# Start of an adapter kernel: block 0's tokens in four loads, its B rows in two gathered halves, row numbers on Pool

## The chip, the core and the metric

The kernel runs on one core of one Trainium2 chip. A core has five engines that run their own instruction streams and meet at semaphores: TensorE (PE, with its weight loads listed apart as PEld), VectorE (DVE), ScalarE (ACT), GpSimd (POOL) and SyncE (SP). Loads and stores are issued by SP or, for gathers through a table of row numbers, by POOL. All of them are carried out by the same 16 DMA engines. The metric is the time of one execution on the device in microseconds (us).

## What is computed

4096 tokens (64 sequences of 64), each of 1024 features, pass two residual layers in float32. The first adds a rank-16 adapter chosen for each sequence. The second adds a dense product with W and a mixture of eight rank-16 adapters with the two best gates.

```python
def reference(x, itok_B_4_50, itok_B_0_7, L0_cond_A, L0_cond_B,
              L1_cond_W, L1_cond_Wr, L1_cond_A, L1_cond_B):
    # layer 0: per sequence, its own adapter
    Bx  = einsum('bni,bri->bnr', x, B0[ids0])
    x   = x + einsum('bnr,bor->bno', Bx, A0[ids0])          # SCALING 1
    # layer 1
    base   = einsum('btd,od->bto', x, W)
    logits = einsum('btd,ed->bte', x, Wr) + 5.0 * one_hot(ids1)
    gates  = softmax over the 2 largest logits, 0 elsewhere
    h      = einsum('btd,erd->bter', x, A1)
    lora   = einsum('bter,bte,eor->bto', h, gates, B1)
    return x + base + 2.0 * lora
```

## The kernel before

Tokens lie along the free axis (`xT` is features by tokens), in 8 blocks of 512 tokens. A block `k` has two tiles of 1 MB, `("x", k, 0)` and `("x", k, 1)`, each with four chunks of 128 features (`HC` = 4). Blocks are taken in pairs. For a pair, the product with W plus the identity is a fast matrix multiplication of seven products at two levels (`products`, lines 817 to 1043), which fills nearly all of TensorE's time.

Before that, each block goes through a preparation, written as small functions:

- `load` (line 366): SP loads the block's two token tiles. `gather` (line 400): POOL gathers 128 rows (eight sequences of rank 16) of B (`gb`) and of A (`ga`) by an indirect DMA, 512 KB each, with row numbers `idx` (line 294).
- `turn` (line 415): TensorE transposes the gathered B in two groups of four 128x128 pieces (`pt`), and ScalarE copies each group to `bt`.
- `project` (line 436): TensorE multiplies `bt` with the tokens (`pb`), in two steps, one for each token tile. VectorE masks the sum into `bx`.
- `adapt` (line 468): TensorE makes the adapter's output (`px`) from `bx` and `ga`, and VectorE adds it to the tokens in place, eight operations a block.
- `rows` (line 506): TensorE makes hidden rows and logits (`ph`) from the tokens and `a1_sb`; then `gates` on VectorE and `weigh` (`pg`) follow.

The first three words of a block's preparation, `turn`, `project` and `adapt`, are called `early`; `rows`, `gates` and `weigh` are `late`.

Nothing of this is issued in the order in which it is written. Each function hands steps to a `Plan` (line 34) with the engine, an estimated duration, what is read and written, a due number `at`, and for DMAs a size. `Plan.order` (line 65) runs a small model of the engines and fixes one order for every engine; `Pinned` (line 19) keeps it. Two kinds of edges exist there: `reads`/`writes` are real dependences, and `behind` only asks that another step has begun. The constants of the model are in lines 44 to 51; `GATHER` is what it adds to a gather's landing. An engine then works in that order and waits in place, so an instruction that waits holds all behind it on its engine.

Two holds are made by hand. A tile's first column is written by a small POOL copy that reads another tile, and the DMA that fills the tile must come after that copy:

```python
pool.tensor_copy(made[t][:, 0, :1], made["x", 0, 0][:, 0, :1])   # line 374: x_0_1's load after x_0_0's first half
pool.tensor_copy(a1_sb[:, 0, :1], made["gb", 0][:, :1])          # line 321: a1's load after the gathered B of block 0
```

SP issues in order, so with `a1`'s load the loads behind it wait as well: the 16 pieces of W (`load_w`, line 637), block 1's tokens and `b1`. Through `behind` block 1's gathers follow too.

In the built program the start stands thus. SP: `ids_sb`, two halves of `x_0_0` (512 KB each), `wr_c`, `ids1_sb`, `x_0_1` (1 MB, waits for POOL's copy), `a1_sb` (waits for POOL's second copy), two pieces of W, `x_1_0`, `x_1_1`, 14 pieces of W, `b1_sb`. POOL: constants, `gb` of block 0, copy for `x_0_1`, `ga` of block 0, copy of `wr_c` into `a1_sb` (line 328), copy for `a1_sb`, `gb` and `ga` of block 1, then sums of weight pieces. TensorE: `pt`, `pb`, `px` of block 0, both groups of `pt` of block 1, `ph` of block 0 (four strips of 128 tokens), `pb` of block 1, then the first product (`pw`) with `px` of block 1 between.

On a second tensor with the same name: the page writes `in_b` for both B tables, `in_a` for both A tables, `ids_sb` for both id tiles, `x` for every token tile and `w` for the pieces of W and for two small gate tiles. All of the kernel's own operations carry line 29, that of the recording helper.

Of the kernel before, what the change touches and what calls it, by code (L numbers as in the profile page):

```python
# [11 lines left out]
ALU = mybir.AluOpType  # L12
AX = mybir.AxisListType

P = 128
# [18 lines left out]
class Plan:  # L34
# [10 lines left out]
    LOOK = 0.2  # L45
    LAND = 1.8
    KB = 350.0
    GATHER = 1.5
    AHEAD = 6.0
    PACE = {"DVE": 0.36, "POOL": 0.73}  # L50
    SET = {"SP": 1.2, "DVE": 3.1, "POOL": 2.9}
# [13 lines left out]
    def order(self):  # L65
# [65 lines left out]
        while ready:  # L131
# [23 lines left out]
            if st["kb"]:  # L155
                moved = max(moved, clock[e]) + st["kb"] / self.KB
                end[n] = (moved if e == "SP" else clock[e] + self.GATHER) + self.LAND
            where[n] = e
# [23 lines left out]
def kernel(  # L182
# [44 lines left out]
    D, NT = xT.shape  # L227
# [7 lines left out]
    TB = 512  # L235
# [3 lines left out]
    RANK = P // BPB  # L239
    NJ = TB // P  # L240
    HC = NC // 2
# [14 lines left out]
    pe, dve = Pinned(tc, nc.tensor), Pinned(tc, nc.vector)  # L256
    act, pool, sp = Pinned(tc, nc.scalar), Pinned(tc, nc.gpsimd), Pinned(tc, nc.sync)
# [6 lines left out]
    plan = Plan(slots, {"l"})  # L264
# [7 lines left out]
    def new(tag, shape, name):  # L272
        return pools[tag].tile(shape, F32, tag=tag, name=name)


    ids_sb = const.tile([P, NBLK], I32, name="ids_sb")
# [5 lines left out]
    rcol = const.tile([P, 1], F32, name="rcol")  # L282
# [8 lines left out]
    dve.tensor_copy(half, half_i)  # L291
    mask = const.tile([P, GT], F32, name="mask")
    idx = const.tile([P, NBLK], I32, name="idx")
    dve.tensor_scalar(idx, ids_sb, float(RANK), rcol, ALU.mult, ALU.add)
    pool.memset(mask[:, :SEQ], 0.0)
    pool.memset(mask[:, SEQ:], float(RANK))

    a1_sb = const.tile([P, NC, P + E], F32, name="a1_sb")
# [10 lines left out]
    dve.tensor_copy(order, order_i)  # L309
    b1_sb = const.tile([P, O], F32, name="b1_sb")  # L310

    def consts():
        plan.add({"SP": 0.4}, lambda e: sp.dma_start(wr_c, wr), [], [("wr_c",)], -53, kb=8)
        plan.add(
            {"SP": 0.4}, lambda e: sp.dma_start(ids1_sb, ids1[0:1, :].to_broadcast([P, NB])),
            [], [("ids1",)], -53, kb=32,
        )

        def hold(e):

            pool.tensor_copy(a1_sb[:, 0, :1], made["gb", 0][:, :1])

        plan.add({"POOL": 0.2}, hold, [(("gb", 0),)], [("a1",)], -56)
        plan.add({"SP": 0.4}, lambda e: sp.dma_start(a1_sb[:, :, :P], a1), [], [("a1",)], -45, kb=512)
        plan.add({"SP": 0.4}, lambda e: sp.dma_start(b1_sb, b1), [], [("b1",)], -29, kb=512, behind=[("a1",)])

        def spread(e):
            pool.tensor_copy(a1_sb[:, :, P:], wr_c)

        plan.add({"POOL": 0.3}, spread, [("wr_c",)], [("wr",)], -45)  # L330
# [24 lines left out]
    made = {}  # L355

    def part(t, cs=range(HC), gs=range(NG)):
        return [(t, c, g) for c in cs for g in gs]
# [7 lines left out]
    def load(k, i, at):  # L366
        t = ("x", k, i)

        held = (k, i) == (0, 1)

        def hold(e):

            made[t] = new("q", [P, HC, TB], f"x_{k}_{i}")
            pool.tensor_copy(made[t][:, 0, :1], made["x", 0, 0][:, 0, :1])


        cuts = ((0, HC // 2), (HC // 2, HC)) if (k, i) == (0, 0) else ((0, HC),)

        def fn(c0, c1):
            if not held and c0 == 0:  # L380
                made[t] = new("q", [P, HC, TB], f"x_{k}_{i}")
            sp.dma_start(
                made[t][:, c0:c1],
                xT[(i * HC + c0) * P : (i * HC + c1) * P, k * TB : (k + 1) * TB].rearrange(
                    "(c p) t -> p c t", p=P
                ),
            )

        if held:
            plan.add(  # L390
                {"POOL": 0.2}, hold, part(("x", 0, 0), [0]), part(t), at, [("q", t)]
            )
        for c0, c1 in cuts:
            plan.add(
                {"SP": 0.5}, lambda e, c0=c0, c1=c1: fn(c0, c1),
                [], part(t, range(c0, c1)), at, [("q", t)] * (not held and c0 == 0),
                kb=256 * (c1 - c0), behind=[("a1",)] * (k == 1) + [(t, 0, 0)] * (c0 > 0),
            )

    def gather(k, tag, table, at):  # L400
        def fn(e):
            made[tag, k] = new(tag, [P, D], f"{tag}_{k}")
            pool.indirect_dma_start(
                out=made[tag, k],
                out_offset=None,
                in_=table,
                in_offset=bass.IndirectOffsetOnAxis(ap=idx[:, k : k + 1], axis=0),
            )

        plan.add(  # L410
            {"POOL": 1.1}, fn, [], [((tag, k),)], at, [(tag, (tag, k))], kb=512,
            behind=[(("x", 0, 1), 0, 0)] * ((tag, k) == ("ga", 0)) + [("a1",)] * (k == 1) + [(("px", 1, 1, 0),)] * (k > 1),
        )

    def turn(k, g, at):

        pt, bt = ("pt", k, g), ("bt", k)

        def fn(e):
            made[pt] = new("l", [P, PER, P], f"pt_{k}_{g}")  # L420
            if g == 0:
                made[bt] = new("bt", [P, NC, P], f"bt_{k}")
            for c in range(PER):
                cc = g * PER + c
                pe.transpose(made[pt][:, c, :], made["gb", k][:, cc * P : (cc + 1) * P], ident)

        def out(e):
            act.copy(made[bt][:, g * PER : (g + 1) * PER, :], made[pt])

        plan.add(  # L430
            {"PE": 0.44}, fn, [(("gb", k),)] + [(bt, 0)] * g, [(pt,)] + [(bt, 0)] * (g == 0), at,
            [("l", pt)] + [("bt", bt)] * (g == 0),
        )
        plan.add({"ACT": 0.6}, out, [(pt,)], [(bt, g + 1)], at)

    def project(k, at):

        pb, bx = ("pb", k), ("bx", k)

        def fn(cs):  # L440
            if cs[0] == 0:
                made[pb] = new("l", [P, GT], f"pb_{k}")
                made[bx] = new("bx", [P, GT], f"bx_{k}")
            for c in cs:
                for gi in range(NG):
                    strip = slice(gi * CG, (gi + 1) * CG)
                    pe.matmul(
                        made[pb][strip, :],
                        made["bt", k][:, c, strip],
                        x_at(k, c)[:, gi * GT : (gi + 1) * GT],  # L450
                        start=(c == 0),
                        stop=(c == NC - 1),
                        tile_position=(0, gi * CG),
                    )

        def out(e):
            dve.tensor_tensor(made[bx], made[pb], mask, ALU.mult)


        for h in range(2):  # L460
            plan.add(
                {"PE": 0.94}, lambda e, h=h: fn(range(h * HC, (h + 1) * HC)),
                [(("bt", k), 1), (("bt", k), 2)] + part(("x", k, h)), [(pb,)] + [(bx,)] * (1 - h),
                at + 0.1 * h, [("l", pb), ("bx", bx)] * (1 - h),
            )
        plan.add({"DVE": 0.3}, out, [(pb,)], [(bx,)], at - 8)

    def adapt(k, h, at):

        px = [("px", k, h, gi) for gi in range(NG)]  # L470

        tags = "aabb" if (k, h) == (0, 1) else "llll"
        x = ("x", k, h)

        def fn(e):
            for gi in range(NG):
                made[px[gi]] = new(tags[gi], [P, HC, GT], f"px_{k}_{h}_{gi}")
            for c in range(HC):
                cc = h * HC + c
                for gi in range(NG):  # L480
                    strip = slice(gi * CG, (gi + 1) * CG)
                    pe.matmul(
                        made[px[gi]][:, c, :],
                        made["ga", k][strip, cc * P : (cc + 1) * P],
                        made["bx", k][strip, :],
                        start=True,
                        stop=True,
                        tile_position=(gi * CG, 0),
                    )

        def out(gi):
            def fn(e):
                xs = made[x][:, :, gi * GT : (gi + 1) * GT]
                dve.tensor_tensor(xs, made[px[gi]], xs, ALU.add)

            return fn

        plan.add(
            {"PE": 1.1}, fn, [(("ga", k),), (("bx", k),)], [(t,) for t in px], at,
            list(zip(tags, px)),  # L500
        )
        for gi in range(NG):
            xs = part(x, gs=[gi])
            plan.add({"DVE": 0.62}, out(gi), [(px[gi],)] + xs, xs, at - 2 + 1.5 * gi * (k == 0))
# [172 lines left out]
    POOL = {"POOL": 1.25}  # L677
# [366 lines left out]

    for k, at in ((0, -60), (1, -42)):
        load(k, 0, at)
        gather(k, "gb", b0, at - 1)
        load(k, 1, at)
        gather(k, "ga", a0, at)
        if k == 0:  # L1050
            consts()
# [81 lines left out]
```

## Time and profile before

| | |
|---|---|
| median of 3 runs | 522.11 us (521.61 to 522.37) |
| the profiled execution | 521.59 us |
| its span, first to last instruction | 519.8 us |
| outside the span in that execution | 1.8 us |
| PE busy | 504.9 us, 97% of the span |
| DVE, POOL, ACT busy | 300.9, 170.0, 41.1 us |
| granted TensorE clock | 1.000 |
| HBM read, written | 69.01 MB, 29.62 MB |

A row of a timeline has the start, the duration (merged where several instructions of one kind follow each other), the engine, the operation and its operands, and in brackets the idle time of the engine before it with what ended it. "SPq" is SP's queue issuing a DMA: the duration there is that of the issue, not of the transfer. A row of the chain of waits has start, duration, engine and tile. A row of the table of windows has the stretch, its length, each engine's busy time with the number of instructions, the granted clock, the share of the 16 DMA engines and the rate in GB/s.

Where this document gives the landing of a DMA, it is the last of the 16 completions that the trace records for it. Where it counts packets, these are the trace's DMA packets by queue (queue 0: POOL's gathers; queue 1: SP's loads and stores), time and size.

### The profile page before, as it was taken

To read this page: it belongs to the slowest core of one execution; us is meant where nothing else is said; L and a number is where in the kernel's file an instruction comes from. 1 tells how busy PE (TensorE), PEld (TensorE's weight loads), DVE (VectorE), ACT (ScalarE), POOL (GpSimd) and SP (SyncE) were. 2 spreads that over 40 slices of the span, in tenths; PEclk is the share of its full clock that TensorE was granted. 3 is DMA by queue.
4 is the path that set the end of the run, shared out by engine and by line. 5 is a ranking of instruction groups with operands and counts; after the bars stand their busy time and mean duration, and the time that the engine had idled before them with its cause. 6 is when DMAs were issued, how large, how long until landed. Compare 5 with 4: busy or idle time off the path is not lost.

```text
span 519.8 us, 8542 instructions
## 1 busy us (share of the span) xinstructions
PE 504.9 (97%) x3432; PEld 439.3 (85%) x3432; DVE 300.9 (58%) x572; ACT 41.1 (8%) x81; POOL 170.0 (33%) x141
## 2 busy tenths in 40 slices
PE   2999999999999999999999999999999999999996
PEld 2857988888888988898888998889888898888885
DVE  0699998986953383526684256435486418433632
ACT  1111100002000100012000100000200010000000
POOL 4072067170332144124233313312423322433300
PEclk9999999999999999999999999999999999999999
DMA  7999276799566269716565537744546633610122
GB/s 263 370 367 381 103 263 221 276 326 342 194 202 203 63 194 317 238 61 204 182 224 186 159 101 212 269 149 124 163 161 202 204 95 107 204 62 0 56 104 83
DMA packets 54247, 99.19 MB, mean 191 GB/s; under 512 B 4928, under 2 KB 11072, under 8 KB 54208
## 3 DMA queue, kind: packets, MB, share of 16 engines
q1 hardware_dynamic: 51904, 90.26, 51.6%
q0 software_dynamic: 2304, 8.39, 4.8%
q8 instruction: 27, 0.44, 0.3%
q14 instruction: 12, 0.10, 0.0%
HBM read 69.01 MB, written 29.62 MB: 190 GB/s over the span
## 4 chain that ended last, share of the span: by engine, by line
PE 96%; DMA 2%; DVE 0%; issue 0%; SPq 0%; POOL 0%
PE pa L29 39%; PE pb L29 38%; PE ph L29 11%; PE px L29 3%; PE pw L29 3%; DMA x<-in_xT 2%; PE pt L29 1%; PE pg L29 1%; DVE o L29 0%; SPq L29 0%; DVE bx L29 0%; POOL x L29 0%
## 5 line engine op out<-in xcount | busy, mean ns | idle before, releaser
L29 PE MATMUL pa<-ti,s 128*128 128x256 f32 x432 | 102.5, 380 | 0.0
L29 PE MATMUL pb<-ti,s 128*128 128x256 f32 x384 | 95.8, 380 | 0.0
L29 PEld LDWEIGHTS pa<-ti,s 128*128 128x128 f32 x432 | 80.8, 190 | 11.2 <-issue 0.2
L29 PEld LDWEIGHTS pb<-ti,s 128*128 128x128 f32 x384 | 72.1, 190 | 10.0
L29 PEld LDWEIGHTS ph<-a_sb,x 128*128 128x128 f32 x512 | 62.6, 190 | 1.5 <-issue 0.4
L29 PE MATMUL ph<-a_sb,x 128*128 128x136 f32 x512 | 63.1, 279 | 0.2 <-issue 0.2
L29 POOL TENSOR_TENSOR ti<-x,ti 128x512 f32<-128x512 f32 x24 | 32.2, 1340 | 78.0 <-PE pb L29 77.1
L29 DVE TENSOR_TENSOR o<-pb,o 128x512 f32<-128x512 f32 x47 | 32.4, 690 | 36.1 <-PE pb L29 21.7
L29 PE MATMUL pa<-x,s 128*128 128x256 f32 x216 | 51.9, 379 | 0.0
L29 POOL TENSOR_TENSOR ti<-t,ti 128x512 f32<-128x512 f32 x18 | 25.7, 1429 | 71.0 <-PE pb L29 61.3
L29 POOL TENSOR_TENSOR ti<-x 128x512 f32<-128x512 f32 x24 | 30.8, 1282 | 55.4 <-PE pb L29 41.8
L29 PEld LDWEIGHTS pa<-x,s 128*128 128x128 f32 x216 | 40.1, 190 | 5.3 <-issue 0.3
L29 DVE TENSOR_TENSOR x<-px,x 128x512 f32<-128x512 f32 x64 | 39.8, 684 | 6.8 <-PE px L29 6.8
L29 PE MATMUL pa<-t,s 128*128 128x256 f32 x168 | 41.0, 380 | 0.0
L29 POOL TENSOR_TENSOR ti<-t 128x512 f32<-128x512 f32 x18 | 24.4, 1358 | 42.9 <-PE pb L29 33.4
L29 PEld LDWEIGHTS pa<-t,s 128*128 128x128 f32 x168 | 31.6, 190 | 4.5 <-issue 0.4
L29 DVE TENSOR_TENSOR o<-pa,u 128x512 f32<-128x512 f32 x32 | 22.0, 688 | 20.8 <-PE pa L29 20.1
L29 DVE TENSOR_TENSOR u<-pb,u 128x512 f32<-128x512 f32 x21 | 14.5, 689 | 25.1 <-ACT u L29 20.7
L29 POOL TENSOR_TENSOR s<-w,w 128x512 f32<-128x512 f32 x12 | 17.0, 1418 | 36.0 <-DVE w L29 36.0
L29 PE MATMUL pb<-hg,b_sb 128*128 128x256 f32 x96 | 28.6, 379 | 0.0
L29 DVE TENSOR_TENSOR o<-pa,v 128x512 f32<-128x512 f32 x15 | 10.3, 690 | 25.9 <-PE pa L29 25.9
L29 DVE TENSOR_TENSOR v<-pa,u 128x512 f32<-128x512 f32 x16 | 11.0, 689 | 22.3 <-PE pa L29 22.1
(113 smaller groups left out, 609.5 us busy)
## 6 DMA issues: line engine op xcount, KB each, us to landing
s<-s_kept SPq DMA_DIRECT2D x147, 256.0 KB
x<-in_xT SPq DMA_DIRECT2D x15, 1024.0 KB
out_T<-o SPq DMA_DIRECT2D x30, 512.0 KB
s_kept<-s SPq DMA_DIRECT2D x28, 256.0 KB
s_kept<-w SPq DMA_DIRECT2D x18, 256.0 KB
w<-in_w SPq DMA_DIRECT2D x16, 256.0 KB
x<-in_xT SPq DMA_DIRECT2D x2, 512.0 KB
out_T<-o SPq DMA_DIRECT2D x4, 256.0 KB
```

What stands on the lines that cost most here:

```text
L29: return self._tc.keep_in_program_order(f(*args, **kwargs))
```

## The change

Block 0's second token tile is no longer held; both tiles come in halves, so that four loads of 512 KB stand behind each other on SP. The hold on `a1_sb` reads the last half of `x_0_1` instead of the gathered B. Block 0's B is gathered by two indirect DMAs, one for each half of the columns (256 KB each), and each group of transposes depends on its own half alone. `idx` is computed by POOL, as its last operation before the gathers. `GATHER` goes from 1.5 to 2.3.

```diff
-    GATHER = 1.5
+    GATHER = 2.3
...
-    dve.tensor_scalar(idx, ids_sb, float(RANK), rcol, ALU.mult, ALU.add)
...
+    pool.tensor_scalar(idx, ids_sb, float(RANK), rcol, ALU.mult, ALU.add)
+
     def consts():
...
-            pool.tensor_copy(a1_sb[:, 0, :1], made["gb", 0][:, :1])
-
-        plan.add({"POOL": 0.2}, hold, [(("gb", 0),)], [("a1",)], -56)
+            pool.tensor_copy(a1_sb[:, 0, :1], made["x", 0, 1][:, HC // 2, :1])
+
+        plan.add({"POOL": 0.2}, hold, part(("x", 0, 1), [HC // 2]), [("a1",)], -56)
...
     def load(k, i, at):
         t = ("x", k, i)
-        held = (k, i) == (0, 1)
-        def hold(e):
-            made[t] = new("q", [P, HC, TB], f"x_{k}_{i}")
-            pool.tensor_copy(made[t][:, 0, :1], made["x", 0, 0][:, 0, :1])
-        cuts = ((0, HC // 2), (HC // 2, HC)) if (k, i) == (0, 0) else ((0, HC),)
+        cuts = ((0, HC // 2), (HC // 2, HC)) if k == 0 else ((0, HC),)
...
     def gather(k, tag, table, at):
-        def fn(e):
-            made[tag, k] = new(tag, [P, D], f"{tag}_{k}")
+        n = 2 if (tag, k) == ("gb", 0) else 1
+        def fn(h):
+            if h == 0:
+                made[tag, k] = new(tag, [P, D], f"{tag}_{k}")
             pool.indirect_dma_start(
-                out=made[tag, k],
+                out=made[tag, k][:, h * D // n : (h + 1) * D // n],
                 out_offset=None,
                 in_=table,
                 in_offset=bass.IndirectOffsetOnAxis(ap=idx[:, k : k + 1], axis=0),
+                element_offset=h * D // n,
             )
+        if n == 2:
+            plan.add(
+                {"POOL": 1.1}, lambda e: fn(0), [], [((tag, k), 0)], at, [(tag, (tag, k))], kb=256
+            )
+            plan.add(
+                {"POOL": 1.1}, lambda e: fn(1), [], [((tag, k), 1)], at, kb=256,
+                behind=[((tag, k), 0)],
+            )
+            return
...
-            {"PE": 0.44}, fn, [(("gb", k),)] + [(bt, 0)] * g, ...
+            {"PE": 0.44}, fn, [(("gb", k), g)] + [(bt, 0)] * g, ...
...
-                [(("bt", k), 1), (("bt", k), 2)] + part(("x", k, h)), ...
+                [(("bt", k), h + 1)] + part(("x", k, h)), ...
...
     for k, at in ((0, -60), (1, -42)):
         load(k, 0, at)
+        load(k, 1, at)
         gather(k, "gb", b0, at - 1)
-        load(k, 1, at)
         gather(k, "ga", a0, at)
```

In the built program this gives, on SP: `ids_sb`, four halves of block 0's tokens, `wr_c`, `ids1_sb`, `a1_sb` (waits for POOL), and from there the same loads as before. On POOL: constants, `idx`, two halves of `gb`, `ga`, the copy for `a1_sb` (waits for the last half of `x_0_1`), `gb` of block 1, the copy of `wr_c`, `ga` of block 1. On TensorE the second group of block 1's transposes stands between the two pairs of `ph` strips instead of before them. One store of a weight piece changes places with its neighbour on SP. From there on the orders are the same.

More of the change, by code (lines that the diff above doesn't have):

```diff
@@ L367, in load @@
         t = ("x", k, i)
-        held = (k, i) == (0, 1)
-        def hold(e):
-            made[t] = new("q", [P, HC, TB], f"x_{k}_{i}")
-            pool.tensor_copy(made[t][:, 0, :1], made["x", 0, 0][:, 0, :1])
-        cuts = ((0, HC // 2), (HC // 2, HC)) if (k, i) == (0, 0) else ((0, HC),)
+        cuts = ((0, HC // 2), (HC // 2, HC)) if k == 0 else ((0, HC),)
         def fn(c0, c1):
-            if not held and c0 == 0:
+            if c0 == 0:
                 made[t] = new("q", [P, HC, TB], f"x_{k}_{i}")
@@ L387, in fn @@
             )
[L389 to L392, printed above, removed]
         for c0, c1 in cuts:
@@ L395, in load @@
                 {"SP": 0.5}, lambda e, c0=c0, c1=c1: fn(c0, c1),
-                [], part(t, range(c0, c1)), at, [("q", t)] * (not held and c0 == 0),
+                [], part(t, range(c0, c1)), at, [("q", t)] * (c0 == 0),
                 kb=256 * (c1 - c0), behind=[("a1",)] * (k == 1) + [(t, 0, 0)] * (c0 > 0),
@@ L407, in fn @@
                 in_offset=bass.IndirectOffsetOnAxis(ap=idx[:, k : k + 1], axis=0),
+                element_offset=h * D // n,
             )
+        if n == 2:
[7 more added lines that the diff above has]
+            return
         plan.add(
-            {"POOL": 1.1}, fn, [], [((tag, k),)], at, [(tag, (tag, k))], kb=512,
+            {"POOL": 1.1}, lambda e: fn(0), [], [((tag, k), h) for h in range(2)], at, [(tag, (tag, k))], kb=512,
             behind=[(("x", 0, 1), 0, 0)] * ((tag, k) == ("ga", 0)) + [("a1",)] * (k == 1) + [(("px", 1, 1, 0),)] * (k > 1),
@@ L430, in turn @@
         plan.add(
-            {"PE": 0.44}, fn, [(("gb", k),)] + [(bt, 0)] * g, [(pt,)] + [(bt, 0)] * (g == 0), at,
+            {"PE": 0.44}, fn, [(("gb", k), g)] + [(bt, 0)] * g, [(pt,)] + [(bt, 0)] * (g == 0), at,
             [("l", pt)] + [("bt", bt)] * (g == 0),
@@ L462, in project @@
                 {"PE": 0.94}, lambda e, h=h: fn(range(h * HC, (h + 1) * HC)),
-                [(("bt", k), 1), (("bt", k), 2)] + part(("x", k, h)), [(pb,)] + [(bx,)] * (1 - h),
+                [(("bt", k), h + 1)] + part(("x", k, h)), [(pb,)] + [(bx,)] * (1 - h),
                 at + 0.1 * h, [("l", pb), ("bx", bx)] * (1 - h),
@@ L498, in adapt @@
         plan.add(
-            {"PE": 1.1}, fn, [(("ga", k),), (("bx", k),)], [(t,) for t in px], at,
+            {"PE": 1.1}, fn, [(("ga", k), 0), (("bx", k),)], [(t,) for t in px], at,
             list(zip(tags, px)),
```

## The prediction

> **What bounds the kernel now.** I read the chain of waits first. It is TensorE nearly everywhere, and only two pieces of it are not, both loads of block 0's tokens at the very start:
>
> ```profile
> 1.19 3.33 DMA x<-in_xT
> 4.78 8.80 DMA x<-in_xT
> 18.64 7.65 PE ph L29 x64
> ```
>
> TensorE has 519.8 - 504.9 = 14.9 us without work, 9.7 of them before its first transpose, and none that I found between 18.6 and 46 us. So whatever time this change wins or loses shows as a shift of the first `ph`, at 18.64, unless something later swallows it. Next I read the timeline of the first 20 us:
>
> ```profile
> 2.36 0.23 DVE L29 TENSOR_SCALAR idx<-ids_sb,rcol 128x8 int32<-128x8 int32 x1 [0.77 <-DMA ids_sb<-in_ids]
> ...
> 2.88 1.11 POOL L29 DMA_INDIRECT gb<-in_b,idx  x1 [1.11 <-DVE order L29]
> ...
> 4.92 0.97 POOL L29 DMA_INDIRECT ga<-in_a,idx  x1 [0.16 <-issue]
> 6.45 0.24 POOL L29 COPY a_sb<-wr_c 128x64 f32<-128x64 f32 x1 [0.56 <-DMA wr_c<-in_wr]
> 9.64 0.18 POOL L29 COPY a_sb<-gb 128x1 f32<-128x1 f32 x1 [2.95 <-DMA gb<-in_b,idx]
> ...
> 9.72 1.94 PE L29 MATMUL pt<-ident,gb 128*128 128x128 f32 x8 [9.72 <-DMA gb<-in_b,idx]
> 9.85 0.65 SPq L29 DMA_DIRECT2D a_sb<-in_a  x1
> 9.97 0.97 POOL L29 DMA_INDIRECT gb<-in_b,idx  x1
> ...
> 11.59 1.54 PE L29 MATMUL pb<-x,bt 128*32 128x128 f32 x32
> ...
> 13.72 1.08 PE L29 MATMUL pb<-x,bt 128*32 128x128 f32 x32 [0.59 <-DMA x<-in_xT]
> ```
>
> Two waits run side by side: the gathered B (issued 2.88, landed 9.59) lets `pt` begin, and the second token tile (issued 4.78, landed 13.59) lets the second half of `pb` begin, 0.59 us after TensorE was ready for it. The table of windows shows what the second tile lost:
>
> ```profile
> 5.00:6.00 1.00, 0.00 (x0) 0.00 (x0) 0.00 (x0) 0.00 (x0) 0.89 (x1) 1.00 0.74 156
> 6.00:7.00 1.00, 0.00 (x0) 0.00 (x0) 0.00 (x0) 0.00 (x0) 0.24 (x1) 1.00 0.45 80
> 7.00:8.00 1.00, 0.00 (x0) 0.00 (x0) 0.00 (x0) 0.00 (x0) 0.00 (x0) 1.00 0.77 248
> 8.00:9.00 1.00, 0.00 (x0) 0.00 (x0) 0.00 (x0) 0.00 (x0) 0.00 (x0) 1.00 0.96 383
> ```
>
> The last column is GB/s. Between 3 and 5 us it is 393 and 408, after 9 about 406. The hold leaves a hole of 244 + 320 + 152 KB, about 1.8 us of full traffic.
>
> **The change, part by part.**
>
> *Row numbers on POOL.* `idx` took 0.23 us on DVE, and the gather began 0.29 us after its end. On POOL its nearest rows are 0.18 us (copy of 128x1) and 0.24 us (copy of 128x64); begun at 2.36 it ends near 2.6. The gain is between 0 and 0.25 us; I take 0, the first half starting at 2.85, because POOL's other gathers also begin 0.16 to 0.3 us after what precedes them. DVE loses nothing behind `idx`: `mask` and `order` are wanted only at 14.8.
>
> *Token loads without a hold.* `x_0_1` goes out as two issues of 0.46 us each from about 2.1 instead of at 4.78. `wr_c` and `ids1` stand 0.9 us later on SP; their users (POOL's copy, now behind block 1's `gb`, and DVE at 21.24) have time. By 3.0 us 0.18 MB had moved. Tokens, the small loads and block 0's B are 2.69 MB; the rest at 400 KB/us ends at 9.3. I add 0.6 us because a gather's first packets are slow (the 128 of `gb` took 10 us more than at their usual 159 ns, over 16 engines), 0.7 for a part of `ga` between, 0.3 from last packet to completion: landed at 10.9, against 13.59. Bounds: 8.3 if the gathers stay behind (tokens and small loads alone, (2.16 - 0.18)/0.4 = 5.0 after 3.0, plus 0.3), 12.2 if all of `ga` goes first with the 0.7 us by which the engines of this load finished apart.
>
> *Two half gathers.* An indirect DMA holds POOL for 0.94 to 1.11 us, a row for each partition whatever its length, with 0.3 us between two. So: first half 2.85 to 3.95, second 4.2 to 5.2, `ga` 5.5 to 6.5 instead of 4.92 to 5.88. Landing after the end of the issue: 5.6 us here, 5.4 and 5.8 for the next two B gathers with loads queued beside them, 3.1 and 3.2 for the two fastest of the run (136.8 and 216.7 us). The first half has 128 packets of half the size, so 0.6 us less (8 per engine at 159 against 84 ns): I take 5.0, landed 8.9. The second is behind it in one queue: 16 packets' time of 84 ns alternating with tokens, 1.35 us, lands 10.2. Bounds: 8.4 (3.2 after its issue) to 11.8 (2.9 after the first, the largest of the distances 2.9, 1.9, 1.9 at which later gathers follow each other). `ga` follows by about 2.5, at 12.7; `px` wants it after 14.
>
> One rule speaks against this part. The Trainium skill, "DMA: Bandwidth & Descriptors", section "Anatomy of one DMA — SWDGE (gpsimd) path", gives each gather a fixed 2.0 us beside its bytes. By it (an estimate from that page) the second half would land 2.6 us after the first, at 11.5, and the change would win nothing here; the 1.9 us between whole gathers in this trace says that they overlap.
>
> *TensorE up to `px`.* The first group of `pt` starts at 8.95 and is done before the second half lands. From there: second group 0.88 (10.78 to 11.66 before), first half of `pb` 1.54, so the second half of `pb` starts at 10.25 + 2.42 = 12.7 instead of 13.72. It has its tokens since 10.9. From its start to the first `ph` without a wait: 1.48 to `px`, 2.07 of `px`, 0.6 for four transposes = 4.2 us, so `ph` at 16.9 at the earliest.
>
> *The hold moved to the tokens.* The copy waits on POOL until 10.9 instead of 9.59. Queued behind it on POOL are block 1's `gb`, the copy of `wr_c`, block 1's `ga`; on SP `a1`, all of W and block 1's tokens. `a1` goes out at 11.15 (before 9.85), `gb` of block 1 from 11.3 to 12.25 (before 9.97 to 10.94, landed 16.32). TensorE meets that gather before `ph`, in order, so it is late next. Its first packet follows the issue by 1.05 us (block 0's), and it landed 3.3 us after its first packet: 16.5. Bounds: 15.3 (fastest rows) to 18.0 (6.7 from its start, the slowest B gather). With 0.1 to start, 0.55 for the four transposes and 0.05, `ph` starts at 17.2. One group of transposes (0.55) now comes later, so the shift that counts is 18.64 - 17.2 - 0.55 = 0.9 us won; 2.1 and -0.6 at the bounds. `a1` took 7.5 us to land with 0.5 MB of tokens before it; without them I expect 16 to 17, just early enough.
>
> *The loads behind the hold.* They leave 1.3 us later but find the engines empty: `a1`'s first packets could flow at 12.2, where the last engine had come to them at about 13.2. So they are between 1.3 later and 1.0 earlier, and I take 0.5 earlier. This has a consumer without slack:
>
> ```profile
> 27.98 0.49 DVE L29 TENSOR_TENSOR w<-w,ident 128x128 f32<-128x128 f32 x2
> ...
> 40.27 2.48 DVE L29 TENSOR_TENSOR x<-px,x 128x512 f32<-128x512 f32 x4
> ```
>
> The piece of W that the first of these needs landed at 27.95. DVE is then busy without a gap to the end of the second (42.75), and block 1's second `px` on TensorE, at 43.34, needs that. So TensorE can win 0.6 us plus what W comes earlier: 1.1.
>
> *`GATHER`* moves one group of transposes (counted) and a store; nothing else.
>
> **Sum.** Three limits: tokens and B 18.64 - 16.9 - 0.55 = 1.2, block 1's B 0.9, W 1.1. Nearly equal; I take 1.0. The profiled execution of 521.59 becomes 520.6; its run lies 0.5 under the median, so from 522.11 the prediction is 521.1 us. 0.2% is 1.04 us, about what a measurement of this kernel tells from no change, so the forecast lies at that edge.
>
> **Rivals.** *No gain at the start:* the tokens crowd out the gathers, the second half lands at 11.3 or later, or W comes no earlier than now. For: the three slow B gathers had loads beside them. Against: with loads queued, gathers took 17 packets of 4 KB per 0.25 us to the loads' 12 of 2 KB (near 43 us). Time: the first limit gives 0.1, the third 0.6; about 521.8.
>
> *Slower: block 1's B stands in TensorE's way.* The hold releases it 1.3 us later. If it needs 8.0 us from its start, as block 1's gather of A did (11.24 to 19.28), it lands at 19.3, `ph` starts at 20.0, and 1.9 us are lost: 524.0. It decides from a landing of 17.4 on, where the gain is zero. For: it also gets the whole of `a1` and W beside it. Against: that gather stood behind two others, and this one has only `ga` before it.
>
> *Earlier than thought:* gathers at their fast rows (second half 8.7, block 1's B 15.4) and tokens at 9.5: about 2 us, 520.1.
>
> That the change does not do what it says I leave out: the order of the built program has the four loads, the halves and the hold as written.
>
> **How the numbers follow.** Forecast 0.54 (gain 0.5 to 1.7), no gain 0.26, slower rival 0.13, earlier 0.07. Of the forecast two thirds lie beyond 1.04 us: faster 0.36 + 0.07 = 0.43. The rest of it, the no-gain case and a third of the slower rival are within 0.2%: 0.18 + 0.26 + 0.04 = 0.48, and slower is 0.09; since the late gather is bounded only by rows of other places, I move 0.04 to slower. The range takes the bounds: 2 us won to 0.7 lost, a little past the slow bound of block 1's B: 520.1 to 522.8. The forecast's own range is 520.4 to 521.6.
>
> **What would show it.** No hole in the rate between 5 and 8 us; `x_0_1` landed near 10.9; two `gb` rows on POOL of about 1 us each; the second half of `pb` near 12.7, waiting for no DMA; the first of block 1's transposes waiting for its gather, near 16.6; `ph` near 17.2; `w<-w,ident` near 27.5. I am wrong if `pt` still starts after 9.7, or if the first `ph` comes after 18.1.

## The result, and the profile after

| | before | after |
|---|---|---|
| median of 14 runs each | 522.23 us (521.39 to 522.93) | 522.31 us (521.04 to 522.96) |
| ratio of the runs, 95% interval | | 1.0001 [0.9993, 1.0009] |
| profiled execution, its span | 521.59, 519.8 us | 522.14, 520.4 us |

No change that can be told: the interval is -0.4 to +0.5 us. The profiled pair differs by 0.55 us, a little more than the medians allow; what follows explains that pair.

The chain of waits of the changed kernel (start, duration, engine and tile) reads differently at the start. Tokens are gone from it, and the gathered B stands in their place:

```profile
3.38 7.10 DMA gb<-in_b,idx
10.48 0.14 issue
10.61 2.13 PE pt L29 x8
12.75 3.09 PE pb L29 x64
...
16.20 2.07 PE px L29 x64
18.27 0.59 PE pt L29 x4
18.86 3.87 PE ph L29 x32
```

The timeline of the same kernel has the details (columns as before):

```profile
2.58 0.27 POOL L29 TENSOR_SCALAR idx<-ids_sb,rcol 128x8 int32<-128x8 int32 x1 [0.81 <-DMA ids_sb<-in_ids]
...
3.38 1.17 POOL L29 DMA_INDIRECT gb<-in_b,idx  x1 [0.53 <-POOL idx L29]
...
4.85 0.95 POOL L29 DMA_INDIRECT gb<-in_b,idx  x1 [0.30 <-issue]
6.11 0.94 POOL L29 DMA_INDIRECT ga<-in_a,idx  x1 [0.30 <-issue]
...
10.61 2.13 PE L29 MATMUL pt<-ident,gb 128*128 128x128 f32 x8 [10.61 <-DMA gb<-in_b,idx]
10.72 0.19 POOL L29 COPY a_sb<-x 128x1 f32<-128x1 f32 x1 [3.66 <-DMA x<-in_xT]
...
11.05 0.97 POOL L29 DMA_INDIRECT gb<-in_b,idx  x1 [0.15 <-issue]
...
12.68 3.10 PE L29 MATMUL pb<-x,bt 128*32 128x128 f32 x64
...
18.20 0.66 PE L29 MATMUL pt<-ident,gb 128*128 128x128 f32 x4
...
18.78 1.40 PE L29 MATMUL ph<-a_sb,x 128*128 128x136 f32 x10
```

Three things are to be seen. The tokens are early, as the change wants: the copy that reads the last half of `x_0_1` runs at 10.72, that half having landed at 10.66 (13.59 before), and `pb` does all its 64 products without a wait for a DMA. But `pt` starts at 10.61 and not at 9.72: the first half of B landed at 10.48, the second at 11.59, though the whole had landed at 9.59 before. And `pb` takes 3.10 us, where its halves took 1.54 and 1.08. The first `ph` is 0.14 us later than before (18.64), and one group of transposes, some 0.45 us, is still to come behind it: together the 0.6 us by which the span is longer. The difference is still there later: block 1's second `px` starts at 43.92 (43.34 before).

The table of windows of the changed kernel (the last two columns are the share of the DMA engines and GB/s):

```profile
5.00:6.00 1.00, 0.00 (x0) 0.00 (x0) 0.00 (x0) 0.00 (x0) 0.80 (x1) 1.00 0.98 238
6.00:7.00 1.00, 0.00 (x0) 0.00 (x0) 0.00 (x0) 0.00 (x0) 0.89 (x1) 1.00 0.98 356
7.00:8.00 1.00, 0.00 (x0) 0.00 (x0) 0.00 (x0) 0.00 (x0) 0.05 (x1) 1.00 0.95 338
...
11.00:12.00 1.00, 1.00 (x6) 0.67 (x5) 0.00 (x0) 0.26 (x1) 0.94 (x1) 1.00 0.62 254
12.00:13.00 1.00, 1.00 (x12) 0.65 (x14) 0.00 (x0) 0.54 (x2) 0.83 (x3) 1.00 0.22 53
```

The hole between 5 and 8 us (156, 80 and 248 GB/s before) is mostly filled, and a new one stands between 11 and 13. What the hold on `a1` keeps back flows no earlier than before: the first packet of `a1` comes at 12.38 us (11.91 before), the hundredth at 13.08 (12.39). So W gains nothing; the piece that landed at 27.95 lands at 28.00.

The gather's first packet in the trace's packet records tells where the gathered B is lost: it comes at 8.15 us, 3.60 after the end of its issue (4.55); before, at 5.33, 1.34 after the end (3.99).

### The profile page after: what moved, and what is told of

Its sections match the earlier page's. It is cut to its first block, busy times and chain, and to the rows that moved or that the text cites. A ratio compares the mean times of both kernels' runs of the same rounds, so it can differ in the third digit from the quotient of the medians.

```text
span 520.4 us, 8545 instructions
## 1 busy us (share of the span) xinstructions
PE 505.3 (97%) x3432; PEld 439.8 (85%) x3432; DVE 299.8 (58%) x571; ACT 41.1 (8%) x81; POOL 171.5 (33%) x142
## 4 chain that ended last, share of the span: by engine, by line
PE 97%; DMA 2%; DVE 0%; issue 0%; POOL 0%; POOLq 0%
PE pa L29 39%; PE pb L29 38%; PE ph L29 11%; PE px L29 3%; PE pw L29 3%; PE pt L29 2%; DMA gb<-in_b,idx 1%; PE pg L29 1%; DMA ids_sb<-in_ids 0%; DVE o L29 0%; DVE bx L29 0%; POOL idx L29 0%; POOLq L29 0%
```

## The experiments

Ratios are to the kernel before on the same chip; its medians there are 522.07 us (first four runs below), 521.46 (`e_only_loads`, `e_window`, `e_warm`, `e_warm_before`) and 521.71 (`e_only_split`, `e_warm_again`, `e_early`, `e_best`). Edits are to the changed kernel where nothing else is said.

**The changed kernel again.**

> The changed kernel as it is, a second profile beside the others. If the start is decided by an order of queues (queue theory: block 0's gathers do not flow while token packets stand in SP's queue), its marks come back within 0.3 us: first packets of the gathers near 8.0, first half of B landed near 10.5, second near 11.6, first ph near 18.8. If they are chance (memory latency at the start), they move by a microsecond between the two profiles. Time the same as before, within 0.1%.

522.45 us, 1.0002 [0.9992, 1.0011]. First packet 7.99, halves of B landed 10.42 and 11.34. So the late B is no accident of one execution. The first `ph` comes at 19.17, 0.39 later than in the first profile although B is a little earlier, because `pb` takes longer:

```profile
12.43 3.64 PE L29 MATMUL pb<-x,bt 128*32 128x128 f32 x64
```

The last section says what this is: TensorE's rate doubles only at 16.74 us here, at 15.08 in the first profile.

**Row numbers on VectorE as before.**

```diff
+    dve.tensor_scalar(idx, ids_sb, float(RANK), rcol, ALU.mult, ALU.add)
...
-    pool.tensor_scalar(idx, ids_sb, float(RANK), rcol, ALU.mult, ALU.add)
```

> The row numbers go back to VectorE, all else as changed. The first half gather is issued at 2.9 instead of 3.4, the second at 4.3, A's at 5.5. Issue theory (a gather lands a fixed 5.9 us after its issue ends, so late issue is what cost the gain): first half lands at 10.0, second at 11.1, first ph at 18.3, 0.5 us faster than the changed kernel. Queue theory (the gather flows when the tokens have drained): first gather packets stay near 8.0, first half stays at 10.3 to 10.5, ph stays near 18.7, time unchanged within 0.1%.

522.25 us, 1.0003 [0.9993, 1.0013]. The issue starts at 2.88 again, 0.50 earlier, and the first packet comes 0.73 earlier (7.42); yet the halves land at 10.28 and 11.21, only 0.2 to 0.4 us earlier than after, and `ph` starts at 18.82. So `idx` on POOL costs half a microsecond of issue, and nothing that can be told in the end: the later issue is not what makes B late.

**One gather instead of two halves.**

```diff
-        n = 2 if (tag, k) == ("gb", 0) else 1
+        n = 1
```

> Block 0's B gathered by one DMA of 512 KB again, all else as changed. Queue theory: its packets begin near 8.0 as well and it lands 0.3 to 0.6 before the second half did, at 11.0 to 11.3; all eight transposes wait for it, so pt starts at 11.2, the second half of pb at 14.7, ph at 19.3: 0.5 us slower than the changed kernel. Split theory (the second DMA's fixed cost is what hurts): it lands at 10.3 and ph comes at 18.4, 0.4 us faster.

523.42 us, 1.0022 [1.0013, 1.0031]. B landed whole at 11.36, between the two halves of the changed kernel, `px` starts at 17.42 (16.20) and the time is 1.0 us above the changed kernel's in the same set. With the tokens unheld, the split wins 1 us.

**512 KB more of tokens behind block 0's.**

```diff
+    spare = const.tile([P, 2, TB], F32, name="spare")
...
+        plan.add(
+            {"SP": 0.5},
+            lambda e: sp.dma_start(
+                spare, xT[: 2 * P, 7 * TB : 8 * TB].rearrange("(c p) t -> p c t", p=P)
+            ),
+            [], [("spare",)], -60, kb=512, behind=[(("x", 0, 1), HC // 2, 0)],
+        )
```

> 512 KB of other tokens are loaded right behind block 0's into a tile that nobody reads; all else as changed. Queue theory: the gathers' first packets move back by the time of 512 KB, from 8.0 to about 9.3, first half lands at 11.7, second at 12.9, ph at 20.0, time 1.2 us more. Issue theory: the gathers' packets stay near 8.0, first half stays at 10.5 and the time moves by less than 0.5 us (a1 and what is behind it leave no later, since the hold is on block 0's tokens alone).

522.94 us, 1.0017 [1.0007, 1.0026]; its load is read by nobody, and the order behind the first `ph` differs, so only the start is compared. The first packet comes at 8.11, where it came at 8.15 without the load. A gather that waited until all queued loads had run would have come past 9. B landed only 0.35 us later, `ga` 1 us. So the wait ahead of the first packet does not go on growing with what is queued; that simple theory falls.

**The kernel before with the tokens unheld, nothing else.**

```diff
-        held = (k, i) == (0, 1)
+        held = False
-        cuts = ((0, HC // 2), (HC // 2, HC)) if (k, i) == (0, 0) else ((0, HC),)
+        cuts = ((0, HC // 2), (HC // 2, HC)) if k == 0 else ((0, HC),)
```

> The kernel before with one part of the change: block 0's second token tile unheld, in two halves. Window theory (tokens already queued on the engines when a gather is announced go first, 84 ns a packet on each engine; tokens queued later share with it): 648 packets are left when the gather's issue ends at 4.0, 40 an engine, so its first packet comes at 7.4 instead of 5.3, it lands near 11.0 instead of 9.6, pt starts at 11.1, ph at 19.4 to 19.9, 0.8 to 1.3 us slower than before. Rival (only the half gathers or the late row numbers moved it): it lands at 9.6 to 10.0, the wait for tokens is gone and ph comes at 18.2, 0.4 us faster.

523.47 us, 1.0038 [1.0025, 1.0051]: 2 us slower, and the first `ph` comes 1.6 us later (20.24). Its timeline:

```profile
2.88 1.11 POOL L29 DMA_INDIRECT gb<-in_b,idx  x1 [1.11 <-DVE order L29]
...
10.88 1.94 PE L29 MATMUL pt<-ident,gb 128*128 128x128 f32 x8 [10.88 <-DMA gb<-in_b,idx]
...
12.74 3.64 PE L29 MATMUL pb<-x,bt 128*32 128x128 f32 x64
```

The gather is the same instruction at the same time as before (2.88), and its first packet comes at 7.26 instead of 5.33, its landing at 10.74 instead of 9.59. This is the cleanest view of the price: two more token loads queued ahead make a gather 1.2 us late. The other 0.4 us at `ph` arise on TensorE, whose `pb` runs all through at the half rate of the last section. `e_only_loads`, `e_window` and `e_warm_before` ran on one chip, so the times of 3.27, 2.28 and 1.26 us from the end of the issue to the first packet (four, three and two loads ahead) are no difference of chips.

**The kernel before with the gather split, nothing else.**

```diff
+        n = 2 if (tag, k) == ("gb", 0) else 1
...
-            {"PE": 0.44}, fn, [(("gb", k),)] + [(bt, 0)] * g, ...
+            {"PE": 0.44}, fn, [(("gb", k), g)] + [(bt, 0)] * g, ...
...
-            pool.tensor_copy(a1_sb[:, 0, :1], made["gb", 0][:, :1])
+            pool.tensor_copy(a1_sb[:, 0, :1], made["gb", 0][:, D // 2 : D // 2 + 1])
```

> The kernel before with the split of block 0's B alone: two gathers of 256 KB, transposes and pb on their own halves, a1 held by the second half of B; tokens held as before, idx on VectorE. Theory (no part alone is worth anything, because tokens and B end at nearly the same time): first packet near 5.4 as before, halves landed near 8.3 and 9.8, pt near 8.4, but x_0_1's load is released by POOL only behind the second gather, near 5.4 (4.78 before), and lands near 14.0; second half of pb there, ph near 18.9, median 0.2 to 0.5 us over the kernel before. Rival (the split is worth 1 us wherever it stands, as e_whole against the changed kernel): ph near 17.7, median 1 us under it.

525.48 us, 1.0077 [1.0054, 1.0100]: 3.8 us slower, far worse than expected. Its chain of waits shows why:

```profile
5.28 0.20 POOL x L29
...
5.49 9.88 DMA x<-in_xT
15.37 0.14 issue
15.51 1.97 PE pb L29 x32
...
17.85 3.38 PE px L29 x64
...
22.60 3.48 PE ph L29 x28
```

The copy that releases `x_0_1` waits on POOL behind the second gather, so the load goes out at 5.49 (4.78 before) and lands at 15.37 (13.59). That is 1.8 us of the 3.96 by which `ph` is later: 0.7 by the later issue, and 1.1 by the transfer itself (9.88 us for 8.80), which no run takes apart; `a1`, now released by the second half of B, goes out earlier beside it (8.98 for 9.85). The other 2.2 are TensorE's own: the second half of `pb` takes 1.97 us (1.08 before) and `px` 3.38 (2.07). The same products take nearly twice as long, as if at half the clock; the trace's own clock record begins only at 20.65, and between the halves of `pb` TensorE had stood still for 3.76 us. Neither part of the change is good alone: the split as built here delays the tokens through POOL, and the unheld tokens without the split cost 2 us (1.35 in `e_whole`, where the hold of `a1` reads the tokens and `idx` is on POOL).

**The second half of `x_0_1` held by VectorE** until the first half of `x_0_0` is there (and row numbers on VectorE).

```diff
+            if (k, i) == (0, 1) and c0:
+                dve.tensor_copy(made[t][:, c0, :1], made["x", 0, 0][:, 0, :1])
             sp.dma_start(
```

> The changed kernel with the row numbers on VectorE and the fourth token load held, by a one-column copy on VectorE, until the first has landed (4.5): three loads unheld, none missing for long. Window theory: at 4.0 some 390 token packets are left, 24 an engine, so the first gather packet comes at 6.1, the first half of B lands at 9.0 to 9.3, the second near 10.2, ph at 17.5, about 0.9 us faster than the changed kernel. Rival (a gather beside any queue of tokens starts 3.4 us after its issue): first packets at 7.4, first half at 10.3, time as with the row numbers on VectorE alone, 522.2.

Median 521.94 us, 1.0028 [1.0010, 1.0046]: seven of twelve runs between 521.5 and 522.0, the others between 522.9 and 526.4, why these I can't say. Its timeline:

```profile
4.87 0.15 DVE L29 COPY x<-x 128x1 f32<-128x1 f32 x1 [1.74 <-DMA x<-in_xT]
...
8.72 1.08 PE L29 MATMUL pt<-ident,gb 128*128 128x128 f32 x4 [8.72 <-DMA gb<-in_b,idx]
...
10.68 1.12 PE L29 MATMUL pt<-ident,gb 128*128 128x128 f32 x4 [0.88 <-DMA gb<-in_b,idx]
...
11.73 3.37 PE L29 MATMUL pb<-x,bt 128*32 128x128 f32 x64
...
17.83 0.63 PE L29 MATMUL pt<-ident,gb 128*128 128x128 f32 x4 [0.28 <-DMA gb<-in_b,idx]
```

With three loads ahead instead of four the first packet comes at 6.54, 2.28 after the end of the issue, and the first half of B lands at 8.58: this is the early `pt` of the prediction. Two new limits keep the gain from TensorE. The second half lands two microseconds after the first and both groups of `pt` stand ahead of `pb` in TensorE's order; and block 1's B, issued at 11.68 behind the hold on `a1`, makes TensorE wait at 17.83, the next wait the prediction had named.

**TensorE started early**, by 56 transposes of the identity that nobody reads, on the changed kernel and on the kernel before.

```diff
+    def warm(e):
+        made["warm"] = new("l", [P, PER, P], "warm")
+        for i in range(56):
+            pe.transpose(made["warm"][:, i % PER, :], ident, ident)
+    plan.add({"PE": 0.1}, warm, [], [(("warm",), 0)], -100, [("l", ("warm",))])
```

> The changed kernel with 56 transposes of the identity into a PSUM tile that nobody reads, first on TensorE from about 1.5 us, so that its clock is up when block 0's B lands; all other orders as changed. Clock theory (the second half of pb took 1.55 us instead of 1.08 because TensorE's full clock came at 15.1 instead of 12.6): the first pt group goes from 1.0 to 0.5 us, all of pb from 3.1 to 2.0, bx at 14.3 instead of 15.9, ph at 17.3 (block 1's B, landed 16.6, then decides); 1.2 to 1.5 us faster than the changed kernel. Rival (late landings alone set the start): ph within 0.3 us of 18.8, time unchanged.

> The same 56 transposes in the kernel before. There the second half of pb waits for tokens landing at 13.6, whatever the clock: pt and the first half get faster but ph stays at 18.3 to 18.6, time 0 to 0.3 us less than before. If the clock counted alike in both, it would win 1 us or more here too.

> e_warm once more (the changed kernel with 56 identity transposes first on TensorE), because the profiled execution of e_warm was its slowest and had stalls of the instruction stream in pb. Theory (TensorE at half clock costs the changed kernel about 0.5 us in pt and pb): median 0.5 to 0.9 us under the changed kernel's, a typical execution with pb in 2.2 us (3.10 in the changed kernel) and px near 15.3. Rival (the low median of e_warm was chance): median within 0.2 us of the changed kernel's 522.3.

On the changed kernel the medians are 520.96 us, 0.9994 [0.9982, 1.0005], and in a second set 521.20, 0.9992 [0.9979, 1.0004]. On the kernel before it is 521.78, 1.0007 [0.9995, 1.0020]. The timeline of the second set's profile:

```profile
1.54 8.32 PE L29 MATMUL warm<-ident 128*128 128x128 f32 x56 [1.54 <-POOL ident masks.py:199]
10.26 0.66 PE L29 MATMUL pt<-ident,gb 128*128 128x128 f32 x4 [0.41 <-DMA gb<-in_b,idx]
11.66 0.66 PE L29 MATMUL pt<-ident,gb 128*128 128x128 f32 x4 [0.75 <-DMA gb<-in_b,idx]
12.25 1.50 PE L29 MATMUL pb<-x,bt 128*32 128x128 f32 x45
14.06 0.86 PE L29 MATMUL pb<-x,bt 128*32 128x128 f32 x19 [0.31 <-issue]
15.30 2.07 PE L29 MATMUL px<-bx,ga 32*128 32x128 f32 x64 [0.38 <-DVE bx L29]
...
17.88 3.94 PE L29 MATMUL ph<-a_sb,x 128*128 128x136 f32 x32
```

A group of four transposes takes 0.66 us; in the changed kernel eight took 2.13. `pb` takes 2.67 us with a gap of 0.31 in it, which is put down to issue, against 3.10; `px` and `ph` start 0.90 us earlier than in the changed kernel (16.20, 18.78), and block 1's second `px` at 43.02 (43.92). In the first set's profile (`e_warm`), its slowest run, there are three such gaps in `pb`, up to 0.59 us between weight loads; `px` comes only at 16.52 and `ph` at 19.85, so the low time is not seen in that trace.

In the kernel before the same trick is worth nothing (one of its eleven runs took 2401.3 us, from a cause that the record does not show):

```profile
13.44 1.08 PE L29 MATMUL pb<-x,bt 128*32 128x128 f32 x32 [1.29 <-DMA x<-in_xT]
14.93 2.07 PE L29 MATMUL px<-bx,ga 32*128 32x128 f32 x64 [0.40 <-DVE bx L29]
...
19.17 1.05 PE L29 MATMUL ph<-a_sb,x 128*128 128x136 f32 x7 [1.00 <-DMA a_sb<-in_a]
```

The first half of `pb` is done earlier and TensorE then waits for the tokens; the 0.27 us that `px` still gains (15.20 before) are lost to a wait for `a1`, and `ph` is 0.53 us later than before.

**Towards a better one.** `e_early` is `e_window` with block 1's B gathered right behind block 0's A, and the first half of `pb` between the groups of `pt`. Block 1's transposes are kept behind `px`. `e_best` adds the 56 transposes, and holds `a1` by the first half of `x_0_1` (the last two lines).

```diff
-            behind=... + [("a1",)] * (k == 1) + ...
+            behind=... + [("a1",)] * ((tag, k) == ("ga", 1)) + ...
...
+            if (k, h) == (0, 1):
+                turn(k, 1, at - 2)
...
-        turn(k, 1, at)
+        if k:
+            turn(k, 1, at)
...
-            pool.tensor_copy(a1_sb[:, 0, :1], made["x", 0, 1][:, HC // 2, :1])
+            pool.tensor_copy(a1_sb[:, 0, :1], made["x", 0, 1][:, 0, :1])
```

> As in e_window (idx on VectorE, second half of x_0_1 held by x_0_0's first half), and two waits more taken away: block 1's B is gathered right behind block 0's A instead of behind the hold of a1, and TensorE does the first half of pb between the two groups of pt; both groups of block 1's transposes stand behind px, as in the kernel before. Theory (what stood in the way of e_window's early B was first the order pt, pt, pb, then block 1's B at 17.70): halves of B landed near 8.6 and 10.7, first half of pb near 9.9, second near 12.7, px near 14.5 (15.49 in e_window), block 1's B landed before 15, first ph near 17.9 (18.64 before, with as much work in front of it), median 0.5 to 0.7 us under the kernel before. Rival (a start that comes earlier is swallowed later, by W's pieces landing at 28): ph at 17.9 all the same, but block 1's second px still at 43.3 and the time within 0.2 us of the kernel before. Rival (the added gather takes packets from block 0's): second half of B at 11.3 or later, no gain.

> e_early with 56 transposes of the identity ahead of the first pt on TensorE (their result isn't used) and a1's load held by the first half of x_0_1 (landed near 8.5 to 9.4) instead of the second. Theory: pb and pt of block 0 run at full clock (1.08 us for each half of pb), px near 13.8, first ph near 17.2; a1 goes out near 9.5, so W's first pieces land up to 1 us before 28; block 1's second px near 42.2 and the median 1.0 to 1.3 us under the kernel before. Rival (W's pieces or VectorE's chain behind them cap it): block 1's second px not before 42.7, gain 0.6 or less. Rival (the extra 56 instructions cost as much as the clock gives, through stalls of the instruction stream as in the profile of e_warm): gaps put down to issue in pb, no better than e_early.

Both missed. `e_early`: 524.64 us, 1.0062 [1.0041, 1.0083]; first half of B at 9.0 instead of 8.6, and `pt` and the first half of `pb` at half clock with two waits of 0.68 us for ScalarE's copy between them: `ph` at 19.46. At 47.42 TensorE has done what the changed kernel has done at 47.29, so most of its loss comes later and is not explained. `e_best`: 523.18 us, 1.0026 [1.0015, 1.0038], although its `px` is the earliest of all:

```profile
9.05 0.61 PE L29 MATMUL pt<-ident,gb 128*128 128x128 f32 x4
10.33 1.08 PE L29 MATMUL pb<-x,bt 128*32 128x128 f32 x32 [0.68 <-issue]
...
14.17 2.07 PE L29 MATMUL px<-bx,ga 32*128 32x128 f32 x64 [0.41 <-DVE bx L29]
...
18.15 7.65 PE L29 MATMUL ph<-a_sb,x 128*128 128x136 f32 x64 [0.79 <-DMA a_sb<-in_a]
```

`px` comes 2 us before the changed kernel's, `ph` then waits for `a1`, and at 46.12 TensorE has done what the changed kernel has done at 47.29. Then the lead goes: TensorE waits 0.59 us for VectorE's work on a weight piece before 64.69, and its chain of waits enters TensorE at 73.67 from POOL's sum of weight pieces. The edit also changed the order that the plan fixes for what follows, so I can't say how much of the loss is this order and how much the weight pieces, which land no earlier.

## Why the prediction came out as it did

The predicted time of 521.1 us is not what came. Both signs by which it would be wrong came: `pt` started after 9.7 (10.61) and the first `ph` after 18.1 (18.78). That 522.3 still lies in the stated range is luck, since the range's slow end was set by a late landing of block 1's B, which did not come. The case that came is the first rival, "no gain at the start": the second half of B landed at 11.59, past the 11.3 that it named, and W came no earlier. Its time of 521.8 leaves out what TensorE's rate costs, the third step below. Step by step:

| step | predicted | after |
|---|---|---|
| first half of B issued | 2.85 | 3.38 |
| `x_0_1` landed | 10.9 | 10.66 |
| first half of B landed | 8.9 | 10.48 |
| second half, behind the first | 1.3 | 1.11 |
| `ga` landed | 12.7 | 12.84 |
| second half of `pb` starts, no DMA waited for | 12.7 | 14.39 |
| from there to `px` | 1.48 | 1.81 |
| from `px` to `ph` | 2.67 | 2.58 |
| block 1's B issued, landed | 11.3, 16.5 | 11.05, 16.61 |
| first `ph` | 17.2 | 18.78 |
| VectorE's `w<-w,ident` that was at 27.98 | near 27.5 | 28.55 |

*Right:* that the tokens land some 3 us earlier and let the moved hold go near 10.9, the distance of the halves, and that the two halves keep `pb` from waiting. The Trainium skill, "DMA: Bandwidth & Descriptors", section "Anatomy of one DMA — SWDGE (gpsimd) path", gives each gather a fixed 2.0 us; paid one after the other, as in the prediction's estimate from that page, they would have set the halves 2.6 apart. They were 1.11 apart here and 2.06 in `e_window`, and splitting won 1.0 us, so the measurement decides for the overlap, though not always for as much of it.

*Right in the number, by luck in the way:* three landings. `x_0_1` at 10.66 for 10.9: the sum let the tokens give way to gathers and move at 400 GB/s otherwise, but no gather packet moved before 8.15, and from 5 to 8 us the tokens alone moved at 238, 356 and 338. `ga` at 12.84 for 12.7: it came 1.25 us behind the second half of B, not 2.5, and that half was 1.4 us late. Block 1's B at 16.61 for 16.5: its first packet came 2.19 us after the end of its issue, and it landed 2.4 after that, where the sum had 1.05 and 3.3. That 1.05 is also misread: the records of the kernel before show 1.34 for block 0's gather (3.99 to 5.33). And a half of B moves as 64 packets of 4096 bytes, not as 128 of half the size; for the sum this makes no difference.

*Wrong, first step:* "Landing after the end of the issue ... I take 5.0, landed 8.9". It was 5.93 after an issue that itself ended 0.6 late. The landings of the trace of before were taken for a property of the gather, and they are one of the queue it meets. The time from the end of the issue to the first packet, over the profiles: 1.26 to 1.62 us with two token loads queued ahead (before, `e_warm_before`, `e_only_split`), 2.28 to 2.63 with three (`e_window`, `e_best`, `e_early`), 3.25 to 3.90 with four (the seven others), 3.61 with five (`e_more_tokens`). The token packets that had begun by then tell the same: 510 of the 512 queued ahead (before), 714 of 768 (`e_window`), 834 of 1024 (`e_only_loads`), 937 of 1024 (the changed kernel), 953 of 1280 (`e_more_tokens`). So the first packet comes late in the queue each time, but not at its end: 2 packets of it had still to begin with two loads, 54 with three, 190 and 87 with four, 327 with five. All loads are of 512 KB, so whether loads or bytes count is not tested. The prediction let the tokens pay for the gathers ("I add 0.6 us because a gather's first packets are slow"), and it was the gather that paid. Why a gather waits, and why the wait stops growing at four loads, is not shown. The Trainium skill, "DMA: Bandwidth & Descriptors", section "Queues, rings and completion order", says that a DMA engine takes turns between its queues, packet by packet; by that alone a new queue would get its turn at once however many loads stand in another, and `e_only_loads` against the kernel before does not agree: 5.33 against 7.26.

*Wrong, second step:* "*Row numbers on POOL.* ... I take 0". On POOL the gather began 0.53 us after `idx`, on VectorE 0.29, and `idx` itself started at 2.58 rather than 2.36. The cost was 0.5 us of issue, outside the bounds of 0 to 0.25 won; `e_dve_idx` shows that it had no effect on the time.

*Wrong, third step:* "From its start to the first `ph` without a wait: 1.48 to `px`". The row of 1.08 us for the second half of `pb` was a row at full clock: the trace's own clock record begins at 12.59 there, within the first half of `pb` and 2.9 us after the first transpose. In the changed kernel it begins at 15.08, 4.5 us after the first transpose: the first half of `pb` takes 1.71 us (1.54 in the prediction), and the second, 14.39 to 15.78 in the records of single products, takes 1.39. In `after_again` all of `pb` is slow. `e_warm_again` takes this away and wins 0.9 us at `ph`, with both halves of B landed within 0.3 us of the changed kernel's times.

*The sum:* the predicted 17.2 holds 0.38 us by which block 1's B would have held TensorE past the 16.82 of block 0's path (10.25 + 2.42 + 1.48 + 2.67). To 16.82 come 1.34 for the second half of B (11.59 for 10.25), 0.38 from its landing to the second half of `pb` (2.80 for 2.42, of which 0.17 in the first half of `pb`), and 0.33 from there to `px`; less 0.09 from `px` to `ph` this gives 18.78. The two parts in `pb`, some 0.5 us, are the clock's in this profile. The third limit, W, was wrong too (0.5 earlier expected, 0.05 later measured, for the new hole at 11 to 13 us), but nothing reached it.

## What to carry to other kernels

In this kernel the time from a gather's issue to its landing depends on what is queued when it is issued: before loads are released ahead of a gather, count them, and hold back the ones that are needed last, on an engine that isn't busy issuing the gather. Take a TensorE duration from a row only with the clock of that moment: a product that moves nearer to the first work, or behind a wait of some microseconds, may take twice as long. Testing each part of a change alone is worth its runs: here one part costs 2 us, another 3.8, and the whole nothing.

## What the runs showed that was not expected

*Half clock at the start.* In the trace's records the starts of transposes stand 214 ns apart at first and 109 later, and in the packed products of `pb` four take about 215 ns and then 110. The change came between 2.8 and 6.2 us after TensorE's first work in the profiles without a long wait, and in `e_only_split`, with its wait of 3.76 us, 12.9 us after. This is called half clock here because the products take twice as long; the only other value in the trace's clock record is 0.5, behind the last work (at 521.17 in the kernel before). The profile's clock column shows 1.00 in all this time, so it can't be read from there; it has to be read from the durations. The Trainium skill, "TensorE: Matmul & The Clock Gate", section "Part 1: The HAM clock gate (the "warmup" mystery)", gives half clock until about 3.4 us of sustained work have filled a window that runs freely; the spread here fits a free window, and its figure alone would be 0.7 to 2.8 us too short for eleven of the thirteen profiles without a long wait.

*A version that may be faster than both:* the changed kernel with TensorE started early was 0.5 us under the kernel before in both sets (520.96 to 521.46, 521.20 to 521.71). In the second set's trace block 1's second `px` comes 0.90 us before the changed kernel's and 0.32 before that of the kernel before. Each interval just includes no change, so a gain is likely, not shown.
